# Seven products instead of eight for the output projections of six batches, with all transfers issued by SyncE

## The chip, the core and the metric

The program runs on one core of a Trainium2 chip. The metric is the device time in microseconds of one execution. Three runs of the kernel before gave 1334.11, 1334.73 and 1335.27 us, a median of 1334.73 us. One more execution was taken with the hardware profiler, and all durations below come from it.

Five engines matter here. PE (TensorE) multiplies matrices and writes only to PSUM; PEld is the part of it that loads the stationary operand. DVE (VectorE) and ACT (ScalarE) read and write PSUM and SBUF. POOL (GpSimd) does element-wise work on SBUF only. SP (SyncE) issues transfers. Each engine works through its own instructions in order.

## The reference

Two layers run one after the other on x of shape (8, 512, 512), all in float32. The first is a graph attention over the first 20 tokens of each batch. The second is a self-attention with 16 heads, and the change is in its output projection:

```python
h = _sln(hidden, w, ln_g, ln_b, Wg, bg, Wb, bb)          # conditioned layer norm
qkv = (h @ Wqkv.T + bqkv).reshape(B, N, num_heads, hd, 3)
...
energy = jnp.einsum('bhqd,bhkd->bhqk', q, k)
att = jax.nn.softmax(energy, axis=-1) / D ** 0.5
out = jnp.einsum('bhqk,bhkd->bhqd', att, v)
out = jnp.moveaxis(out, 1, 2).reshape(B, N, D)
out = out @ Wp.T + bp                                    # the output projection
h1 = out + hidden
h2 = _sln(h1, w, ln_g, ln_b, Wg, bg, Wb, bb)
return h2 + h1
```

Here B = 8, N = D = 512, and a head has hd = 32 columns.

## The kernel before

**Stages.** The first layer takes the first 412 us and writes its result to the DRAM tensor `mid`. In it `out_weights` (L435) makes a small tensor per direction and half of the batches, and writes it to the DRAM tensor `vo_d` in four pieces (L448, issued by POOL, 16 pieces in all); `load_vo` (L450, issued by SP) reads it back, 20 pieces per batch. The second layer then takes one batch after the other.

**Steps.** The work of the second layer is a list `steps` (L789). For the batches b = 0 to 6 there are 16 steps, one for each group g of four heads and each block c of 128 queries; `at` (0 to 15) is the number of the step in its batch. A step does, in the order in which the code issues it: the scores of the next step (`scores`, L799, PE) and their row maxima (`tops`, L806, DVE); in steps 1 to 4 the transposition of a quarter of the next batch's tokens (`turn`, tile `pz`); in even steps the products of probabilities and values of two steps (`weigh`, tile `pao`); the exponentials of the next step (`exps`, L811, ACT); the transpositions of this step's probabilities in four parts (`turn_probs`, L824, tile `pt`, three copied out by ACT and one by DVE); a first and a second "job"; and the normalization of the next step's probabilities in two pairs (`normalize`: a reciprocal on DVE at L816, then the scaling of two 128x512 tiles on POOL at L819). In DVE's order each reciprocal stands behind the addition that empties the job before it. The transpositions, the jobs and `turn` share three PSUM banks (`bank`, L651).

**Jobs.** `JOBS` (L869) gives each batch 32 slots, two per step, written out by hand; `None` leaves a slot empty. A job is one of these: half of a group of the plain projection of batch 0 (`own`); one of seven products (`product`, L695) that make Q, K or V of the next batch by the Winograd form of Strassen's method; a product of this kind that is done late (`late`); or one of eight blocks of an output projection (`project`, L731). A product is four matmuls with 256 moving columns. So is one block of `project`: 128 tokens by 256 outputs, summed over four blocks of the 512 inputs, and then added to the residual `XQ[b]` by DVE (L742). The batches 1 to 5 have 29 jobs and three empty slots each: the second slots of the steps 8, 10 and 12. The projection of batch b-1 is done in the steps 1 to 4 of batch b.

**Sums for the products.** Winograd's form needs four sums of quarters of each operand. `weight_sums` (L674) makes those of the weights for V, Q and K once, in the steps 0 to 11 of batch 0, on DVE. `token_sums` (L684) makes those of the tokens in every batch, on POOL, in the steps 2, 4, 4 and 5 (in batch 0 in 3, 4, 4 and 5) at the end of the step.

**The end of a batch.** The last norm of batch b-1 is taken in batch b, in four blocks of 128 tokens, at the steps that `FINISH` (L880) gives: "statistics" (DVE, and a power on POOL) in the steps 2, 3, 4 and 5; "norm" (two operations on DVE, L754 and L755) and "sums" (two additions on POOL, L758 and L759, and the transfer to `out` by SP, L760) in the steps 4, 6, 6 and 8. After that, `fetch` loads the residual of batch b+2 into the buffer that has come free. The bias of the projection is added to the residual by POOL (L115) in the steps 10, 11, 12 and 15.

**Tiles.** `outputs` (L842, ACT) writes the attention's outputs `AO[b, g]` to six tiles of 128x512 (pool `aop`, L642).

Of the kernel before, what the change touches and what calls it, by code (L numbers as in the profile page):

```python
# [9 lines left out]
F32 = mybir.dt.float32  # L10
# [3 lines left out]
ALU = mybir.AluOpType  # L14
# [4 lines left out]
B, N, F = 8, 512, 512  # L19
P = 128  # L20
C = N // P
# [3 lines left out]
NG = 20  # L25
# [4 lines left out]
BH = B // 2  # L30
# [14 lines left out]
def graph_then_self_attention(ctx: ExitStack, tc: tile.TileContext, x, x_t, near, near_t, labels, w_self_t, wq, wk_t,  # L45
                              wout_t, wg_t, wb_t, wqkv_t, wp_t, cols, gate_vecs, rows, out):
    nc = tc.nc
# [27 lines left out]
    turned = ctx.enter_context(tc.tile_pool(name="turned", bufs=2))  # L75
# [12 lines left out]
    XQ, Z, HT, Q, K, V, AO, GATE, STATS, PAIRS = {}, {}, {}, {}, {}, {}, {}, {}, {}, {}  # L88
# [79 lines left out]
    with ExitStack() as l0:  # L168
# [9 lines left out]
        def bank(name):  # L178
            return ps.tile([P, 512], F32, tag="bank", name=name)
# [142 lines left out]
        for k in range(C):  # L322
            for f in range(C):
                o = psk[f // 2][:, f % 2, :2 * MH]
# [16 lines left out]
        first = self_feat_main(0, (0,))  # L341
# [34 lines left out]
        made = kv.tile([P, C, HM], F32, tag="kv", name="made").rearrange("p c m -> p (c m)")  # L376
        nk = B * HG * D2
        kqb = made[:4, 0:nk]
        for d in range(2):
            for g2 in range(2):  # L380
                pk = pair(f"pk_{d}_{g2}")
                for g in (2 * g2, 2 * g2 + 1):
                    o = pk[:, g % 2, :2 * MH]
                    for k in range(C):
                        nc.tensor.matmul(o, WK[d][:, k, g * P:(g + 1) * P], sfk[:, k, :], start=(k == 0), stop=(k == C - 1))
                for g in (2 * g2, 2 * g2 + 1):
                    o = pk[:, g % 2, :2 * MH]
# [47 lines left out]
        def out_weights(d, half, ks):  # L435
            if 0 in ks:
                PW[d, half] = bank(f"pw_{d}_{half}")
            pw = PW[d, half]
            for k in ks:
                nc.tensor.matmul(pw[:MH, :], sfk[:, k, half * MH:(half + 1) * MH], WO[d][:, k, :], start=(k == 0), stop=(k == C - 1))  # L440
            if C - 1 not in ks:
                return

            vot = BOUT[d] if half else (three if d else two).tile([P, KB, P], F32, tag="t" if d else "wt", name=f"vot_{d}").rearrange(
                "p i n -> p (i n)")[:MH, :F]
            nc.vector.tensor_tensor(vot, pw[:MH, :], BOUT[d], ALU.add)
            for b in range(BH):
                nc.gpsimd.dma_start(vo_d[BH * half + b, d], vot[NG * b:NG * (b + 1), :])  # L448

        def load_vo(b):  # L450
            src = vo_d[b].rearrange("d m f -> (d m) f")
# [88 lines left out]
        for n in range(2 * C):  # L540
            d, f = n % 2, n // 2
# [97 lines left out]

    w1 = ctx.enter_context(tc.tile_pool(name="w1", bufs=1, reuse_waits="tile"))  # L640
    qkp = ctx.enter_context(tc.tile_pool(name="qkp", bufs=3, reuse_waits="tile"))
    aop = ctx.enter_context(tc.tile_pool(name="aop", bufs=6, reuse_waits="tile"))  # L642
    gp = ctx.enter_context(tc.tile_pool(name="gp", bufs=1, reuse_waits="tile"))
    op = ctx.enter_context(tc.tile_pool(name="op", bufs=2, reuse_waits="tile"))
    ep = ctx.enter_context(tc.tile_pool(name="ep", bufs=8, reuse_waits="tile"))
# [12 lines left out]
    bv = w1.tile([P, C], F32, name="bv")  # L658
    hx = ctx.enter_context(tc.tile_pool(name="hx", bufs=1, reuse_waits="tile"))

    M = F // 2
    SUMS = {}
# [5 lines left out]
    def a_(i, p, q):  # L671
        return quarter(W1[i], q, p)

    def weight_sums(i, n):  # L674

        if n == 2:
            SUMS[i, 2] = a_(i, 1, 0)
        else:
            SUMS[i, n] = w1.tile([P, 2, M], F32, name=f"s{n + 1}_{i}")
        x0, x1, how = ((a_(i, 1, 0), a_(i, 1, 1), ALU.add), (SUMS.get((i, 0)), a_(i, 0, 0), ALU.subtract),  # L680
                       (a_(i, 0, 0), a_(i, 1, 0), ALU.subtract), (a_(i, 0, 1), SUMS.get((i, 1)), ALU.subtract))[n]
        nc.vector.tensor_tensor(SUMS[i, n], x0, x1, how)

    def token_sums(b, n):  # L684

        SUMS["t", n] = (qk0.tile([P, N], F32, tag="qk"[n], name=f"t{n + 1}_{b}").rearrange("p (k n) -> p k n", k=2) if n < 2
                        else hx.tile([P, 2, M], F32, tag=f"t{n}", name=f"t{n + 1}_{b}"))
        x0, x1 = ((quarter(HT[b], 0, 1), quarter(HT[b], 0, 0)), (quarter(HT[b], 1, 1), SUMS.get(("t", 0))),
                  (quarter(HT[b], 1, 1), quarter(HT[b], 0, 1)), (quarter(HT[b], 1, 0), SUMS.get(("t", 1))))[n]
        nc.gpsimd.tensor_tensor(SUMS["t", n], x0, x1, ALU.subtract)  # L690


    b_less = w1.tile([P, 2, 2], F32, name="b_less")

    def product(b, i, n):  # L695
# [27 lines left out]
        for dst, src in {2: [((0, 0), (1, 0))], 6: [((1, 0), (1, 0))], 5: [((1, 1), (1, 0))], 3: [((0, 1), (1, 1))],  # L723
# [4 lines left out]
            else:  # L728
                nc.vector.tensor_tensor(c_(*dst), out, c_(*src), ALU.add)

    def project(b, c, n):  # L731

        if c == 0 and n == 0:
            pool, tag, shape = (turned, "turned", [P, C, F]) if b == B - 1 else (gp, "gate", [P, 2, F])
            GATE[b] = pool.tile(shape, F32, tag=tag, name=f"gate_{b}")[:, 0:2, :]
            nc.sync.dma_start(GATE[b], gates[b].partition_broadcast(P))
# [105 lines left out]
    def outputs(n):  # L842

        b, g, c = steps[n]
        last = b == B - 1
        at = slice(c * P, (c + 1) * P)
        if c == (0 if last else C - 1):
            if not last:
                AO[b, g] = aop.tile([P, N], F32, tag="ao", name=f"ao_{b}_{g}")
# [12 lines left out]

    def out_of(*cs):
        return [("project", c, n) for c in cs for n in range(2)]
# [8 lines left out]
    JOBS[B - 2][14:] = (made(v, 3) + made(q, 1, 2) + [None] + made(q, 6, 5) + made(k, 1) + [None] + made(k, 2, 6) + made(q, 3) + [None]  # L873
                        + made(k, 5, 3) + made(q, 4, 7) + made(k, 4, 7))
# [16 lines left out]

    def finish_parts(part):
        for block in FINISH.get((b, at), ()):
            if block[2] == part:
                finish(*block)

    def job(b, slot):
        what = JOBS[b][slot] if slot < len(JOBS[b]) else None
        if what is None:
            return  # L900
        kind, *of = what
        if kind == "own":
            i, f, n = of
            if n == 0:
                OWN[0] = q_or_k(i, f)
            OWN[0].half(n)
        elif kind == "product":
            product(b + 1, *of)
        elif kind == "late":
            product(b, *of)  # L910
        else:
            project(*(of if b == B - 1 else [b - 1] + of))

    with tc.manual_schedule():
# [22 lines left out]
        for n, (b, g, c) in enumerate(steps):  # L937
# [129 lines left out]
```

## Time and profile before

| | us |
|---|---|
| median of three runs | 1334.73 (1334.11 to 1335.27) |
| profiled execution | 1335.18 |
| span of its instructions | 1333.40 |
| first layer, 0 to 412.3 | 412.30, PE busy 404.49 |
| batches 0 to 6, 412.3 to 1226.0 | 813.70, PE busy 811.30 |
| batch 7 (another order of steps), 1226.0 to 1333.4 | 107.40, PE busy 98.96 |

The granted clock of PE is 1.00 in all but the last of these, where it is 0.98. The groups of instructions that the change touches, all with 128 partitions in float32:

| line, engine | what | count | mean ns |
|---|---|---|---|
| L740 PE | block of the output projection, 256 columns | 496 records (two per matmul) | 382 |
| L705 PE | one of seven products for Q, K, V, 256 columns | 1568 records | 379 |
| L742 DVE | adds a block to the residual, 128x256 | 62 | 424 |
| L729 DVE | adds a product to a result, 128x512 | 119 | 688 |
| L690 POOL | sum of two quarters of tokens, 128x512 | 28 | 1271 and 1409 |
| L758, L759 POOL | last sums of a block, 128x512 | 31 each | 1288, 1273 |
| L819 POOL | scales probabilities, 128x512 | 511 | 708 |
| L448 POOL | issues a piece of `vo_d` | 16 | 505 to 539 |

How to read it: a matmul's records overlap the next one's, so their busy times don't add up to the time that they take. The chain of waits (the work that ended last, followed back from the last instruction) gives the time that each group really held the end back; there the four matmuls of a job appear as one piece "x8".

### The profile page before, as it was taken

The page shows a single profiled execution, that of the slowest core. Times are in us where ns is not written, and L with a number is a line of the kernel's source. Part 1 is how long each engine was busy: PE and PEld are TensorE (multiplying, and loading weights), DVE is VectorE, ACT ScalarE, POOL GpSimd, SP SyncE. Part 2 cuts the span into 40 slices and gives each one's busy share as a digit, 9 for nine tenths or more (in the row PEclk, how much of TensorE's full clock was granted, in tenths as well). Part 3 has the DMA queues.
Part 4 walks back from the last instruction along what each step waited for, and adds up shares of the span by engine and source line. Part 5 has one row for each costly group of instructions (what it writes and reads, how often), then busy time and mean ns, then how long its engine had stood idle before and what let it go on. Part 6 is the DMA issues. An engine that isn't in the chain of part 4 may idle for free.

```text
span 1333.4 us, 29328 instructions
## 1 busy us (share of the span) xinstructions
PE 1314.7 (99%) x11251; PEld 967.4 (73%) x11251; DVE 943.7 (71%) x1723; ACT 683.2 (51%) x1664; POOL 755.6 (57%) x865
## 2 busy tenths in 40 slices
PE   8999999999999999999999999999999999999997
PEld 5566666666675677777777777777777777777775
DVE  4567777677646578687677768767776875776887
ACT  1322222222225665656656665665666666566664
POOL 0256654555653555486367548636754864674776
PEclk9999999999999999999999999999999999999999
DMA  9614452253221000001002000100200010010010
GB/s 339 204 64 140 166 191 87 97 159 126 89 74 62 2 2 1 2 25 57 1 10 73 2 1 25 57 2 9 73 2 1 25 57 1 9 41 2 10 41 32
DMA packets 46521, 78.63 MB, mean 59 GB/s; under 512 B 9872, under 2 KB 14416, under 8 KB 46384
## 3 DMA queue, kind: packets, MB, share of 16 engines
q1 hardware_dynamic: 45440, 75.57, 16.7%
q8 instruction: 90, 1.47, 0.5%
q0 software_dynamic: 512, 0.66, 0.2%
q10 hardware_dynamic: 432, 0.55, 0.1%
q14 instruction: 47, 0.39, 0.1%
HBM read 59.27 MB, written 17.49 MB: 58 GB/s over the span
## 4 chain that ended last, share of the span: by engine, by line
PE 86%; DVE 8%; POOL 2%; issue 2%; DMA 1%; ACT 1%; POOLq 0%; SPq 0%; DVEq 0%; ACTq 0%
PE pst L705 18%; PE pt L824 16%; PE s L799 9%; PE pss L471 9%; PE pao L839 8%; PE ppj L740 8%; PE psf L300 6%; PE po L515 2%; PE pqk L138 2%; DVE top L806 2%; PE pz L124 1%; PE ptw L503 1%; PE pw L440 1%; PE pq L421 1%; PE pv L138 1%
## 5 line engine op out<-in xcount | busy, mean ns | idle before, releaser
L819 POOL TENSOR_SCALAR e<-e,den 128x512 f32<-128x512 f32 x511 | 361.6, 708 | 340.5 <-DVE den L816 226.0
L811 ACT ACTIVATE e<-s,top 128x512 f32<-128x512 f32 x512 | 348.6, 698 | 132.2 <-DVE top L806 114.7
L806 DVE TENSOR_REDUCE top<-s 128x2 f32<-128x1024 f32 x256 | 301.1, 1218 | 25.5 <-PE s L799 25.0
L824 PEld LDWEIGHTS pt<-ident,e 128*128 128x128 f32 x2048 | 234.3, 141 | 85.2 <-POOL e L819 32.9
L824 PE MATMUL pt<-ident,e 128*128 128x128 f32 x2048 | 290.8, 277 | 3.7 <-ACT et L826 1.6
L826 ACT COPY et<-pt 128x512 f32<-128x512 f32 x369 | 208.8, 595 | 105.1 <-PE pt L824 103.9
L799 PE MATMUL s<-k_pair,q_pair 32*128 32x512 f32 x992 | 143.7, 640 | 0.9
L471 PE MATMUL pss<-kq,sf 128*128 128x320 f32 x512 | 143.2, 433 | 1.0 <-DVE kq L428 1.0
L839 PEld LDWEIGHTS pao<-et,v 128*32 128x32 f32 x4096 | 107.5, 110 | 44.4 <-issue 44.4
L839 PE MATMUL pao<-et,v 128*32 128x128 f32 x4096 | 126.5, 274 | 0.0
L471 PEld LDWEIGHTS pss<-kq,sf 128*128 128x128 f32 x512 | 94.9, 190 | 37.5 <-ACT sf L307 1.5
L740 PE MATMUL ppj<-w,ao 128*128 128x256 f32 x496 | 118.5, 382 | 0.0
L300 PE MATMUL psf<-vt,ws 128*128 128x512 f32 x256 | 115.0, 593 | 0.0
L811 ACT ACTIVATION_READ_ACCUMULATOR e<-s,top 128x1 f32 x512 | 109.6, 214 | 0.0
L826 DVE COPY et<-pt 128x512 f32<-128x512 f32 x143 | 96.7, 677 | 3.1 <-PE pt L824 2.8
L740 PEld LDWEIGHTS ppj<-w,ao 128*128 128x128 f32 x496 | 89.3, 190 | 12.4 <-ACT ht L126 2.8
L497 POOL TENSOR_TENSOR t<-t,den 128x640 f32<-128x640 f32 x32 | 40.7, 1272 | 81.2 <-DVE den L496 80.6
L300 PEld LDWEIGHTS psf<-vt,ws 128*128 128x128 f32 x256 | 48.3, 190 | 50.7 <-issue 46.6
L505 ACT COPY wt<-ptw 128x640 f32<-128x640 f32 x32 | 22.2, 693 | 104.8 <-PE ptw L503 104.4
L742 DVE TENSOR_TENSOR xq<-ppj,xq 128x256 f32<-128x256 f32 x62 | 26.3, 424 | 69.6 <-PE ppj L740 69.6
L126 ACT ACTIVATE ht<-pz,gates_t 128x512 f32<-128x512 f32 x32 | 24.7, 778 | 74.2 <-PE pz L124 74.2
L492 ACT ACTIVATE t<-t 128x640 f32<-128x640 f32 x32 | 23.6, 737 | 76.1 <-POOL t L489 76.1
(237 smaller groups left out, 1949.0 us busy)
## 6 DMA issues: line engine op xcount, KB each, us to landing
x<-in_x SPq DMA_DIRECT2D x8, 1024.0 KB
mid<-x SPq DMA_DIRECT2D x32, 256.0 KB
xq<-mid SPq DMA_DIRECT2D x8, 1024.0 KB
out<-o SPq DMA_DIRECT2D x31, 256.0 KB
vt<-in_x_t SPq DMA_DIRECT2D x7, 1024.0 KB
labels<-in_labels SPq DMA_DIRECT2D x16, 440.0 KB
wq<-in_wq SPq DMA_DIRECT2D x4, 1024.0 KB
gate<-gates SPq DMA_DIRECT2D x8, 512.0 KB
```

The lines of the kernel that those rows point to most:

```text
L300: nc.tensor.matmul(psf[f], ws[:, k, f * P:(f + 1) * P], VT[b][:, k, :], start=(k == 0), stop=(k == C - 1))
L471: nc.tensor.matmul(o, SF[b][:, k, cut], KQ[b][:, k, on], start=(k == 0), stop=(k == C - 1))
L497: nc.gpsimd.tensor_tensor(tv, tv, den.to_broadcast([P, 2 * H, NG]), ALU.mult)
L705: nc.tensor.matmul(out[:, m, :], fixed[:, k, m * P:(m + 1) * P], moving[:, k, :], start=(k == 0), stop=(k == 1))
L740: nc.tensor.matmul(out, AO[b, k][:, c * P:(c + 1) * P], wp[:, k, on], start=(k == 0), stop=(k == C - 1))
L799: nc.tensor.matmul(S[n][j // 2][:, j % 2, :], Q[b, g][on, c * P:(c + 1) * P], K[b, g][on, :], start=True, stop=True)
L806: nc.vector.tensor_reduce(TOP[n][:, 2 * pair:2 * pair + 2], S[n][pair], AX.X, ALU.max, negate=True)
L811: nc.scalar.activation(e, S[n][pair][:, j % 2, :], AF.Exp, bias=TOP[n][:, j:j + 1], accum_out=DEN[n][:, j:j + 1])
L819: engine.tensor_scalar(E[n][j], E[n][j], DEN[n][:, j:j + 1], att_scale, ALU.mult, ALU.mult)
L824: nc.tensor.transpose(pt[:, k * P:(k + 1) * P], E[n][j][:, k * P:(k + 1) * P], ident)
L826: copy(et, pt.rearrange("p (k n) -> p k n", k=C))
L839: nc.tensor.matmul(PAO[b, g][DH * j:DH * (j + 1), at], V[b][:, k, DH * h:DH * (h + 1)], ET[n, j][:, k, :], start=(k == 0), stop=(k == C - 1))
```

## The change

In the projections of the batches 0 to 5 the eight blocks are replaced by seven products of the Winograd form, of half the rows and half the columns each (`output_product`). Numbers 1 and 5 need only the first two head groups, and are done in the batch itself in step 14; the numbers 2, 3, 6, 7 and 4 are done in the steps 1 to 3 of the next batch. The sums of quarters of the attention's outputs (`output_sums`, POOL) are made in step 10 of the batch and in the steps 1, 2 and 3 of the next; two of them overwrite quarters that are no longer needed. The partial sums that several results share are kept in two tiles `y`; POOL adds them to the residual at the end of the steps 14, 2 and 3 (`add_gathered`). `weight_sums` also makes the sums for the projection's weights, in the steps 12 to 15 of batch 0. `JOBS` is written anew: 31 jobs in batch 0, 28 in the batches 1 to 5 and 26 in batch 6, which had 29 each. The empty slots of the batches 1 to 5 are now the second slots of the steps 0, 4, 10 and 12. The token sums move to the steps 3, 4, 5 and 6, ahead of the first job. The statistics of the last norm move to the steps 5, 5, 6 and 7, its norms and sums to 6, 6, 8 and 8. The 16 writes of `vo_d` move from POOL to SP, and the scratch for transfers that POOL issues is cut to 1024 bytes. Batch 7, and the projections of batches 6 and 7, stay as they were.

```diff
-                nc.gpsimd.dma_start(vo_d[BH * half + b, d], vot[NG * b:NG * (b + 1), :])
+                nc.sync.dma_start(vo_d[BH * half + b, d], vot[NG * b:NG * (b + 1), :])
...
-    aop = ctx.enter_context(tc.tile_pool(name="aop", bufs=6, reuse_waits="tile"))
+    aop = ctx.enter_context(tc.tile_pool(name="aop", bufs=3, reuse_waits="tile"))
...
+    hp = ctx.enter_context(tc.tile_pool(name="hp", bufs=1, reuse_waits="tile"))
...
+    def output_sums(b, n):
+        B12 = quarter_of_outputs(b, 0, 1)
+        x0 = quarter_of_outputs(b, *((0, 1), (1, 1), (1, 1), (1, 0))[n])
+        x1 = (quarter_of_outputs(b, 0, 0), SUMS.get(("o", 0)), B12, SUMS.get(("o", 1)))[n]
+        SUMS["o", n] = B12 if n == 2 else quarter_of_outputs(b, 1, 0) if n == 3 else hp.tile([P, 2, M], F32, tag=f"t{n}", name=f"to{n + 1}_{b}")
+        nc.gpsimd.tensor_tensor(SUMS["o", n], x0, x1, ALU.subtract)
...
+    def add_gathered():
+        for residual, y in TO_ADD:
+            nc.gpsimd.tensor_tensor(residual, y, residual, ALU.add)
+        TO_ADD.clear()
+
+    def output_product(b, n):
...
+        out = bank(f"psp_{b}_{n}").rearrange("p (m n) -> p m n", m=2)
+        for m in range(2):
+            for k in range(2):
+                nc.tensor.matmul(out[:, m, :], t[:, k, m * P:(m + 1) * P], a[:, k, :], start=(k == 0), stop=(k == 1))
...
+        if n in (1, 6, 7):
+            before = Y.get(b)
+            Y[b] = hp.tile([P, 2, M], F32, tag="y", bufs=2, name=f"y{n}_{b}")
+            if n == 1:
+                nc.scalar.copy(Y[b], out)
+            else:
+                nc.vector.tensor_tensor(Y[b], out, before, ALU.add)
+            for at_c in {1: ((0, 0),), 6: ((0, 1),), 7: ((1, 0), (1, 1))}[n]:
+                TO_ADD.append((c_(*at_c), Y[b]))
+        for at_c in {2: ((0, 0),), 3: ((0, 1),), 4: ((1, 0),), 5: ((1, 1), (0, 1))}.get(n, ()):
+            nc.vector.tensor_tensor(c_(*at_c), out, c_(*at_c), ALU.add)
...
-    JOBS = {b: (late + out_of(0, 1, 2, 3) if b else own) + made(v, 1, 2, 6, 5, 3, 7, 4) + [None]
-            + made(q, 1, 2) + made(k, 1) + [None] + made(q, 6, 5) + made(k, 2) + [None] + made(k, 6) + made(q, 3) + made(k, 5, 3)
-            + made(q, 4, 7) + [None] for b in range(B - 1)}
+    first, fifth = [("output", 0, 1)], [("output", 0, 5)]
+    end = made(k, 5, 3) + first + fifth + made(q, 4, 7)
+    JOBS = {0: own + made(v, 1, 2, 6, 5, 3, 7, 4) + made(q, 1, 2, 6, 5) + made(k, 1, 2, 6) + [None] + made(q, 3) + end}
+    for b in range(1, B - 1):
+        JOBS[b] = (late[:1] + [None] + late[1:] + [("output", 1, n) for n in (2, 3, 6, 7, 4)] + made(v, 1) + [None]
+                   + made(v, 2, 6, 5, 3, 7, 4) + made(q, 1, 2, 6, 5) + made(k, 1) + [None] + made(k, 2, 6) + made(q, 3) + [None] + end)
...
-        for block, first, second in (((b - 1, 0), 2, 4), ((b - 1, 1), 3, 6), ((b - 1, 2), 4, 6), ((b - 1, 3), 5, 8)) if b < B - 1 else (
+        for block, first, second in (((b - 1, 0), 5, 6), ((b - 1, 1), 5, 6), ((b - 1, 2), 6, 8), ((b - 1, 3), 7, 8)) if b < B - 1 else (
...
-    SUMS_AT = {True: {3: (0,), 4: (1, 2), 5: (3,)}, False: {2: (0,), 4: (1, 2), 5: (3,)}}
+    SUMS_AT = {3: 0, 4: 1, 5: 2, 6: 3}
+    OUTPUT_SUMS_AT = {1: (1, 1), 2: (1, 2), 3: (1, 3), 10: (0, 0)}
...
+            if at in OUTPUT_SUMS_AT:
+                back, i = OUTPUT_SUMS_AT[at]
+                if 0 <= b - back < B - 2:
+                    output_sums(b - back, i)
+            if at in SUMS_AT and not last:
+                token_sums(b + 1, SUMS_AT[at])
             job(b, 2 * at)
...
-            if b == 0 and at < 12:
-                weight_sums((v, q, k)[at // 4], at % 4)
+            if b == 0:
+                weight_sums((v, q, k, 3)[at // 4], at % 4)
...
             finish_parts("sums")
-            for i in SUMS_AT[b == 0].get(at, ()) if b + 1 < B else ():
-                token_sums(b + 1, i)
+            add_gathered()
+
+            if at == 0 and 0 < b < B - 1:
+                load_gate(b - 1)
...
-    nc = bacc.Bacc("TRN2", target_bir_lowering=False, num_devices=1)
+    nc = bacc.Bacc("TRN2", target_bir_lowering=False, num_devices=1, dynamic_dma_scratch_size=1024)
```

More of the change, by code (lines that the diff above doesn't have):

```diff
@@ L674, in weight_sums @@
     def weight_sums(i, n):
-        if n == 2:
+        if n == 2 and i < 3:
             SUMS[i, 2] = a_(i, 1, 0)
@@ L690, in token_sums, with quarter_of_outputs @@
         nc.gpsimd.tensor_tensor(SUMS["t", n], x0, x1, ALU.subtract)
+    def output_sums(b, n):
[4 more added lines that the diff above has]
+        nc.gpsimd.tensor_tensor(SUMS["o", n], x0, x1, ALU.subtract)
+    def quarter_of_outputs(b, p, q):
+        return AO["pair", b, p][:, :, M * q:M * (q + 1)]
     b_less = w1.tile([P, 2, 2], F32, name="b_less")
@@ L729, in product, with c_, load_gate @@
                 nc.vector.tensor_tensor(c_(*dst), out, c_(*src), ALU.add)
+    Y, TO_ADD = {}, []
+    def add_gathered():
[3 more added lines that the diff above has]
+    def output_product(b, n):
+        a = {1: lambda: a_(3, 0, 0), 2: lambda: a_(3, 0, 1), 3: lambda: SUMS[3, 3], 4: lambda: a_(3, 1, 1),
+             5: lambda: SUMS[3, 0], 6: lambda: SUMS[3, 1], 7: lambda: SUMS[3, 2]}[n]()
+        t = {1: lambda: quarter_of_outputs(b, 0, 0), 2: lambda: quarter_of_outputs(b, 1, 0), 3: lambda: quarter_of_outputs(b, 1, 1),
+             4: lambda: SUMS["o", 3], 5: lambda: SUMS["o", 0], 6: lambda: SUMS["o", 1], 7: lambda: SUMS["o", 2]}[n]()
+        out = bank(f"psp_{b}_{n}").rearrange("p (m n) -> p m n", m=2)
+        for m in range(2):
+            for k in range(2):
+                nc.tensor.matmul(out[:, m, :], t[:, k, m * P:(m + 1) * P], a[:, k, :], start=(k == 0), stop=(k == 1))
+        def c_(p, q):
+            return XQ[b][:, 2 * q:2 * q + 2, M * p:M * (p + 1)]
+        if n in (1, 6, 7):
[9 more added lines that the diff above has]
+            nc.vector.tensor_tensor(c_(*at_c), out, c_(*at_c), ALU.add)
+    def load_gate(b):
+        pool, tag, shape = (turned, "turned", [P, C, F]) if b == B - 1 else (gp, "gate", [P, 2, F])
+        GATE[b] = pool.tile(shape, F32, tag=tag, name=f"gate_{b}")[:, 0:2, :]
+        nc.sync.dma_start(GATE[b], gates[b].partition_broadcast(P))
     def project(b, c, n):
         if c == 0 and n == 0:
[L734 to L736 removed]
+            load_gate(b)
         out = bank(f"ppj_{b}_{c}_{n}")[:, 0:M]
@@ L848, in outputs @@
             if not last:
-                AO[b, g] = aop.tile([P, N], F32, tag="ao", name=f"ao_{b}_{g}")
+                if g % 2 == 0:
+                    AO["pair", b, g // 2] = aop.tile([P, 2, N], F32, tag="ao", name=f"ao_{b}_pair_{g // 2}")
+                AO[b, g] = AO["pair", b, g // 2][:, g % 2, :]
             else:
@@ L861, in made @@
         return [("product", i, n) for n in ns]
-    def out_of(*cs):
-        return [("project", c, n) for c in cs for n in range(2)]
     q, k, v = 0, 1, 2
@@ L868, in graph_then_self_attention @@
     late = [("late", k, n) for n in (4, 7)]
-    JOBS = {b: (late + out_of(0, 1, 2, 3) if b else own) + made(v, 1, 2, 6, 5, 3, 7, 4) + [None]
-            + made(q, 1, 2) + made(k, 1) + [None] + made(q, 6, 5) + made(k, 2) + [None] + made(k, 6) + made(q, 3) + made(k, 5, 3)
-            + made(q, 4, 7) + [None] for b in range(B - 1)}
-    JOBS[B - 2][14:] = (made(v, 3) + made(q, 1, 2) + [None] + made(q, 6, 5) + made(k, 1) + [None] + made(k, 2, 6) + made(q, 3) + [None]
-                        + made(k, 5, 3) + made(q, 4, 7) + made(k, 4, 7))
+    first, fifth = [("output", 0, 1)], [("output", 0, 5)]
[4 more added lines that the diff above has]
+                   + made(v, 2, 6, 5, 3, 7, 4) + made(q, 1, 2, 6, 5) + made(k, 1) + [None] + made(k, 2, 6) + made(q, 3) + [None] + end)
+    JOBS[B - 2][14:] = (made(q, 1, 2) + [None] + made(q, 6, 5) + made(k, 1) + [None] + made(k, 2, 6) + made(q, 3) + [None]
+                        + made(k, 5, 3) + made(q, 4) + [None] + made(q, 7) + made(k, 4) + made(k, 7))
     JOBS[B - 1] = [("late", v, 4), None, ("late", v, 7)]
@@ L910, in job @@
             product(b, *of)
+        elif kind == "output":
+            output_product(b - of[0], of[1])
         else:
```

## Prediction

> **What bounds the kernel.** I read the page's busy shares first, then a table of stretches, one per batch, then the chain of waits of one batch, then the rows of the groups that change.
>
> ```profile
> PE 1314.7 (99%) x11251; PEld 967.4 (73%) x11251; DVE 943.7 (71%) x1723; ACT 683.2 (51%) x1664; POOL 755.6 (57%) x865
> 760.94:877.20 116.26, 116.00 (x1149) 90.60 (x1148) 85.29 (x153) 73.67 (x184) 69.46 (x88) 1.00 0.07 24
> ```
>
> The second line is batch 3 from step 0 to step 15: length, then busy time of PE, PEld, DVE, ACT, POOL, then granted clock, DMA share and GB/s. PE is busy 116.00 of 116.26 us; DVE at 73% and POOL at 60% have room on average. The batches 1 to 6 all take 116.1 to 116.4.
>
> A busy PE need not be the bound. The Trainium skill, "Perfetto Trace Analysis", section "Identifying the Most-Contended Engine", calls matmul occupancy a bad measure and takes the share of weight loads instead: here 90.60 / 116.26 = 78%. By that rule a fifth of PE's time could be hidden waiting, and a job taken out could bring as little as nothing. The old kernel holds the test, because it has steps with two jobs and steps with one. Steps 0 and 10 of batch 3, from the chain of waits (start, length, what):
>
> ```profile
> 760.94 1.07 PE s L799 x8
> 762.01 1.89 PE pao L839 x64
> 763.90 1.02 PE pt L824 x8
> 764.92 1.73 PE pst L705 x8
> 766.65 0.44 PE pt L824 x4
> 767.09 1.73 PE pst L705 x8
> 768.82 0.44 PE pt L824 x4
> ...
> 835.80 1.07 PE s L799 x8
> 836.87 1.89 PE pao L839 x64
> 838.75 1.02 PE pt L824 x8
> 839.78 1.73 PE pst L705 x8
> 841.50 0.87 PE pt L824 x8
> 842.38 1.07 PE s L799 x8
> ```
>
> Step 0 runs from 760.94 to 769.25, 8.31 us; step 10, whose second slot is empty, from 835.80 to 842.38, 6.58. The difference is 1.73, a whole job. So a removed job is worth its full 1.73 us in an even step, and I take the row, not the rule. The odd steps have no `pao` and last 6.43; with `pz` a step is 0.59 longer. From these pieces a batch of before is 8 x (8.31 + 6.43) + 4 x 0.59 - 3 x 1.73 = 115.1; it takes 116.26, so about 1.1 us of waits are left in it.
>
> **The matmuls (the gain).** Slots hold 29 jobs in each of batches 0 to 6, 203 in all; afterwards 31 + 5 x 28 + 26 = 197. A block of the projection and one product are both four matmuls of 256 columns: the chain has 1.73 for `pst` and 1.73 to 1.99 for `ppj` (the 1.99 behind `pz`). A product with an attention output as stationary operand is near the row of `pst` with tokens as stationary operand, so 1.73. Six jobs less: -10.4 us. By batch: +3.46 in batch 0, -1.73 in each of 1 to 5, -5.19 in 6. All empty slots of the new order lie in even steps, where the trace shows the full 1.73; in an odd step with one job (4.7 us) ACT, at 5.1 us a step (four exponentials at 0.67, three copies at 0.6, a share of the rest), would have been the bound.
>
> **DVE.** Out per batch: eight additions of 0.42, 3.4 us. In: products 2, 3, 4, 6 and 7 once and 5 twice over PSUM and SBUF, 7 x 0.69 = 4.8 (the row of L729). 85.3 becomes 86.7 of about 114.5 us, with PE in front. ACT gains one copy of 0.60. Four weight sums of 0.67 come to the steps 12 to 15 of batch 0: in step 12 DVE then has 2.36 (tops) + 3 x 1.0 (norm statistics) + 0.67 + 0.88 + 0.62 + 0.3 = 7.8 against PE's 6.58, made up in the lighter step 13. I charge 0.6 once, between 0 and 1.5.
>
> **The moved norms.** Steps 5, 6 and 8 become fuller on DVE. Step 5 gets a second set of statistics (+1.0); DVE waits 0.4 + 0.4 + 0.15 us for others in that step now, so step 6 starts about 0.1 to 0.4 late. Step 6 already has two norms and loses 0.2 to them:
>
> ```profile
> 815.60 0.03 issue
> 815.62 0.63 PE pt L824 x4
> ```
>
> There the third transposition waits for a bank that DVE empties only after both norms. Step 8 gets the same pair: its first product can be emptied at about 829.9 on the old clock, and its bank is wanted at 822.68 + 5.70 + 0.44 + 1.73 = 830.55. So 0 to 0.4 a batch, and I take 0.1: 0.6 in all.
>
> **POOL.** Eight additions or subtractions of 128x512 come to each of the six batches. The rows:
>
> ```profile
> L690 POOL TENSOR_TENSOR t<-ht,t 128x512 f32<-128x512 f32 x14 | 19.7, 1409 | 0.6
> L759 POOL TENSOR_TENSOR o<-o,xq 128x512 f32<-128x512 f32 x31 | 39.5, 1273 | 2.4
> ```
>
> Two sums at 1.27, two at 1.41 and four additions at 1.27 are 10.4 us a batch: 69.5 becomes 79.9, 70%. None stands on the path if the scaling of probabilities behind it in POOL's order is still in time. The tightest place is step 3 to 4. In step 3 POOL ends its second pair of scalings at about 787.0; then come an addition, an output sum and the token sum, 3.95 us, to 791.0, where the next scaling started at 790.5. It is wanted at 792.40 + 1.07 + 0.59 + 1.88 = 795.9, so the delay is free. In step 4: scalings end at 794.2, two additions and a token sum end at 798.2, the next scaling starts at 799.4. In steps 7 and 9 the four last sums run as they do in step 7 now, without a wait of PE. Output sums 2 and 3 are ready well before their products: number 3 at about 789.7, product 4 starts at 790.2. That is the thinnest margin, 0.5 us; if it is missed, at most the length of one POOL operation, 1.3 us a batch.
>
> A rule speaks against this part. The skill's "SBUF — State Buffer", section "Who interferes with whom", says that POOL shares its port pair with DVE as an exclusive lock, taken by a DVE operation in a two-port mode or with two SBUF inputs, and that the second to come waits in full. The trace agrees that they collide: L754 takes 0.54 us in the median and 1.50 at most, L755 0.69 and 1.06. By the rule alone each of the eight operations could block DVE for 1.27, 10.2 us a batch, and DVE would stand at 97 of 114.5. By the rows a norm loses 0.4 us on average now (means 0.79 and 0.85), and the new operations lie in steps 14, 15, 1 to 4 and 10, the norms in 6 and 8. I add nothing.
>
> **Waits that go or come.** K's third product moves from the second slot of step 14 to step 13, so the scores of the next batch no longer wait for DVE:
>
> ```profile
> 752.14 1.74 PE pst L705 x8
> 753.88 0.03 issue
> 753.91 0.50 DVE k_pair L727
> 754.40 0.04 issue
> ```
>
> The 0.57 includes a transposition of 0.44 that PE does there anyway, so 0.13 a batch is won, 0.8 in all. An empty second slot lets the next step wait about 0.1 for the scaled tile (0.37 after step 12); step 8's goes, step 0's comes under the cover of `pz`: nothing.
>
> **SP.** The 16 writes cost SP 0.34 to 0.62 us each (its other stores of results and of `q_d`). Eight stand ahead of `load_vo(0)`, which began at 53.6 and issues for 8.3; the other eight come behind it, ahead of the load of x for batch 2 at 62.0. That load then starts at 66 to 70. Its reader, a row sum on DVE, starts at 92.9, and `vo` is first read at 86.9; both have 17 us or more. POOL loses 8.3 us of issuing where PE waits for nobody. The residual of batch b+2 is fetched about 1.3 us later, still some 15 us ahead of its statistics. Cost 0; uncovered it would be those few us once.
>
> **Sum.** -10.4 + 0.6 + 0.6 - 0.8 = -10.0. On the profiled execution (1335.2, 1.8 of it outside the span) 1325.2; it lies 0.45 above the median, so **1324.7**.
>
> **Rivals.**
> (a) The fuller stretch gives half of it back. For it: step 6 already waits, and one norm that collides costs 0.96 (1.50 - 0.54). One such loss per batch on PE: 6 x 0.96 = 5.8, so 1330.5. Against it: the colliding norm of step 6 met a token sum, which now comes earlier.
> (b) Slower: POOL becomes the bound from step 1 to step 7. Its scalings are in order behind output sums and additions that wait for products, so a late product holds up the scaling, the transposition and the next product. The added POOL time is 10.4 us a batch; from 1.73 / 10.4 = 17% of it reaching PE on, the change loses. At a third: 6 x (3.5 - 1.73) = +10.6, 1345. Against it: idle stretches of 2 to 5 us ahead of the first scaling in most steps.
> (c) More than the jobs: the remaining waits shrink to 0.5 a batch, -3.6 more: 1321.
> (d) The change does not do what it says: the six products overlap badly because the sums overwrite quarters that are read late, so batches of 28 jobs stay at 116: 1335 + 3.5 - 5 = 1333.
>
> **Chances.** Forecast, within 1322 to 1328: 0.70; (a) 0.12; (b) 0.07; (c) 0.07; (d) 0.04. The range 1320.5 to 1331 takes in (a) and (c). A change under 0.2% (2.7 us) can't be told from none. Faster 0.89 (the first, (a) and (c)), same 0.04, slower 0.07.
>
> **What would show it.** Right: batches 1 to 5 at 114.3 to 114.8, batch 0 near 120, batch 6 near 111; jobs at 1.73; PE still busy above 99% of them. Wrong: waits of `pt` for POOL L819 in steps 1 to 7, `psp` waiting for POOL, or gaps ahead of `pt` in steps 6 and 8. The forecast fails first if one POOL operation a batch comes late.

## The result, and the profile after

Four runs of the changed kernel gave 1322.51 to 1323.78 us, a median of 1322.66; four of the kernel before 1334.99. The ratio is 0.9908, with a 95% interval of 0.9896 to 0.9921: 12.3 us or 0.9% faster. The range of 1320.5 to 1331 held it, and 1322.66 lies inside the 1322 to 1328 that the forecast gave for itself, near the lower edge; the forecast of 1324.7 was 2.0 us too high. The profiled execution took 1322.61 us, with a span of 1320.8.

The page's busy shares, and the same table of stretches as before for batch 0, batch 3 and batch 6 (length, then busy time of PE, PEld, DVE, ACT, POOL, clock, DMA share, GB/s):

```profile
PE 1303.7 (99%) x11203; PEld 959.1 (73%) x11203; DVE 945.8 (72%) x1721; ACT 685.9 (52%) x1670; POOL 811.3 (61%) x897
```

```profile
412.20:530.26 118.06, 117.66 (x1057) 84.25 (x1056) 84.21 (x144) 74.91 (x186) 64.90 (x80) 1.00 0.01 2
758.71:872.94 114.23, 114.14 (x1137) 89.18 (x1136) 85.20 (x152) 74.17 (x185) 79.77 (x96) 1.00 0.07 25
1101.41:1213.19 111.78, 111.31 (x1122) 86.34 (x1121) 78.80 (x134) 73.39 (x184) 75.02 (x90) 1.00 0.04 16
```

Batch 3 went from 116.24 to 114.23 (the table below), and PE is busy in all but 0.09 of it. POOL rose from 69.46 to 79.77 us. The weight loads' share, 89.18 / 114.23 = 78%, is what it was: that number didn't see that PE was the bound, before or after. DVE, which was to rise to 86.7 us, stayed at 85.20: the four norms of batch 3 (L754, L805 in the kernel after) took 2.57 us in all where they took 3.54.

Step 0 of batch 3 lost its second job, and with it the whole 1.73 us (chain of waits: start, length, what). It runs from 758.78 to 765.37, 6.59 us where it took 8.31:

```profile
758.78 1.07 PE s L850 x8
759.85 1.89 PE pao L890 x64
761.74 1.02 PE pt L875 x8
762.76 1.73 PE pst L719 x8
764.49 0.87 PE pt L875 x8
765.37 1.13 PE s L850 x8
```

The lengths of all steps, from the start of one step's scores to the next in PE's timeline, show where the time went. Batch 3 stands for the batches 1 to 5, which agree within 0.02 us a step.

| step | 0 | 1 | 2 | 3 | 4 | 5 | 6 | 7 | 8 | 9 | 10 | 11 | 12 | 13 | 14 | 15 | sum |
|---|---|---|---|---|---|---|---|---|---|---|---|---|---|---|---|---|---|
| batch 0 before | 7.21 | 7.10 | 8.88 | 7.10 | 8.88 | 6.43 | 8.30 | 6.43 | 6.58 | 6.90 | 6.58 | 6.90 | 6.58 | 6.73 | 8.52 | 6.43 | 115.55 |
| batch 0 after | 7.22 | 7.10 | 8.87 | 7.11 | 8.87 | 6.43 | 8.31 | 6.42 | 8.31 | 6.43 | 8.31 | 6.43 | 6.83 | 6.69 | 8.31 | 6.42 | 118.06 |
| batch 3 before | 8.31 | 7.13 | 8.89 | 7.13 | 8.89 | 6.43 | 8.53 | 6.43 | 6.58 | 6.54 | 6.58 | 6.54 | 6.58 | 6.73 | 8.52 | 6.43 | 116.24 |
| batch 3 after | 6.58 | 7.19 | 8.90 | 7.12 | 7.17 | 6.62 | 8.31 | 6.43 | 8.31 | 6.42 | 6.58 | 6.55 | 6.58 | 6.74 | 8.31 | 6.42 | 114.23 |
| batch 6 before | 8.31 | 7.13 | 8.89 | 7.13 | 8.89 | 6.43 | 8.53 | 6.43 | 6.58 | 6.72 | 6.58 | 6.54 | 6.58 | 6.73 | 8.32 | 6.42 | 116.21 |
| batch 6 after | 6.58 | 7.19 | 8.89 | 7.12 | 7.17 | 6.62 | 8.31 | 6.43 | 7.26 | 6.43 | 6.83 | 6.43 | 6.83 | 6.43 | 6.83 | 6.43 | 111.78 |

Batch 0 costs 2.51 us more, the batches 1 to 5 save 2.00 each, batch 6 saves 4.43, and batch 7 is the same. With 0.66 us at the start (the first scores of step 0 begin at 412.20 after 412.86) this is 12.59 us, the difference of the two starts of batch 7 (1225.78 and 1213.19).

### The profile page after: what moved, and what is told of

It reads as the page before. It is cut to its first block, busy times and chain, and to the rows that moved or that the text cites. A ratio compares the mean times of both kernels' runs of the same rounds, so it can differ in the third digit from the quotient of the medians.

```text
span 1320.8 us, 29329 instructions
## 1 busy us (share of the span) xinstructions
PE 1303.7 (99%) x11203; PEld 959.1 (73%) x11203; DVE 945.8 (72%) x1721; ACT 685.9 (52%) x1670; POOL 811.3 (61%) x897
## 4 chain that ended last, share of the span: by engine, by line
PE 87%; DVE 7%; POOL 2%; issue 1%; DMA 1%; ACT 1%; POOLq 0%; SPq 0%; DVEq 0%; ACTq 0%
PE pst L719 19%; PE pt L875 17%; PE s L850 10%; PE pss L471 9%; PE pao L890 8%; PE psf L300 6%; PE psp L762 6%; PE po L515 2%; PE pqk L138 2%; DVE top L857 2%; PE pz L124 1%; PE ptw L503 1%; PE pw L440 1%; PE pq L421 1%; PE pv L138 1%
## 5 line engine op out<-in xcount | busy, mean ns | idle before, releaser
L870 POOL TENSOR_SCALAR e<-e,den 128x512 f32<-128x512 f32 x511 | 366.8, 718 | 262.4 <-DVE den L867 168.3
L477 POOL TENSOR_TENSOR t<-t,mask 128x640 f32<-128x640 f32 x32 | 49.4, 1544 | 33.8 <-issue 30.2
L489 POOL TENSOR_TENSOR t<-t,top 128x640 f32<-128x640 f32 x32 | 40.7, 1273 | 38.4 <-DVE top L488 38.4
L488 DVE TENSOR_REDUCE top<-t 128x32 f32<-128x640 f32 x32 | 26.2, 818 | 44.3 <-POOL t L481 44.2
```

Of the source, the lines that this page charges most:

```text
L477: nc.gpsimd.tensor_tensor(t, t, MASK[b][:, c, None].to_broadcast([P, H, D2]), ALU.mult)
L870: engine.tensor_scalar(E[n][j], E[n][j], DEN[n][:, j:j + 1], att_scale, ALU.mult, ALU.mult)
```

## Experiments

Each ratio compares runs on one chip, and the kernel before took 1335.08 us on the first (`before_sp`, `before_t3`, `before_k3`, `after_odd`), 1335.53 on the second (`after_again`, `after_late_sum`, `after_pool`, `after_slots`) and 1335.13 on the third (`before_t3_late`, `after_again2`, `after_swap`). The step lengths come from each run's own trace.

**Only the transfers.**

```diff
-                nc.gpsimd.dma_start(vo_d[BH * half + b, d], vot[NG * b:NG * (b + 1), :])
+                nc.sync.dma_start(vo_d[BH * half + b, d], vot[NG * b:NG * (b + 1), :])
...
+    nc = bacc.Bacc("TRN2", target_bir_lowering=False, num_devices=1, dynamic_dma_scratch_size=1024)
```

> The kernel before, with only the transfer part of the change: the 16 writes of vo_d issued by SP, the scratch for POOL's transfers cut to 1024 bytes. My theory (the 0.66 us by which the first layer was shorter in the trace of after is chance in the landing of the first load of x_kv): within 0.5 us of before, batches of 116.2 us. Rival (the move to SP takes 0.7 us out of the start by itself): about 1334.2, and x_kv lands at 17.0 us again in place of 17.7.

Measured: 1335.09 us, ratio 1.0000 (0.9992 to 1.0008). The scores of step 0 begin at 413.19, later than in any other trace here (412.20 to 413.12). SP issued the writes and the late load of x in the same order as in the changed kernel (start, length, queue, line, what):

```profile
48.99 4.88 SPq L448 DMA_DIRECT2D vo_d<-vot  x8
54.57 7.63 SPq L458 DMA_DIRECT2D vo<-vo_d  x20
62.30 3.90 SPq L448 DMA_DIRECT2D vo_d<-bout  x8
66.72 0.41 SPq L205 DMA_DIRECT2D x<-in_x  x1
```

The two groups take 0.61 and 0.49 us a write on average, and x starts at 66.7, inside the 66 to 70 of the prediction. Nothing waits for it. The interval alone would still leave room for 0.7 us; the traces do not. With the same transfers the changed kernel itself began step 0 at 412.20, 413.06 and 413.12 in three traces, so the 0.66 us at the start are chance. Which load they come from stays open: x_kv is read from 17.6 us on here, and from 16.7 in the trace that begins step 0 at 413.12, so it is not this load alone. (SP now issues all transfers but the three that ACT issued before and still does.)

**The fourth token sum, moved within POOL's order by nothing.**

```diff
-    SUMS_AT = {True: {3: (0,), 4: (1, 2), 5: (3,)}, False: {2: (0,), 4: (1, 2), 5: (3,)}}
+    SUMS_AT = {True: {3: (0,), 4: (1, 2)}, False: {2: (0,), 4: (1, 2)}}
...
+            if at == 6 and not last:
+                token_sums(b + 1, 3)
             job(b, 2 * at)
```

> The kernel before, with only the fourth token sum moved from the end of step 5 to step 6 ahead of the first job. Theory (step 6 waited 0.22 us because this sum on POOL and the norm on DVE collided, and that is where batches gained more than the job): step 6 falls from 8.53 to 8.31 us in batches 1 to 6, 1.3 us in all, 1333.5; a norm (L754) no longer takes 1.5 us there. Rival (step 6 was relieved by the lighter DVE work of the new job order): step 6 stays at 8.53, 1334.8.

Measured: 1335.12, ratio 0.9999 (0.9991 to 1.0007), and step 6 stayed at 8.53. That looked like the rival's answer, but the trace shows that the edit didn't test it. The timelines of DVE and POOL in step 6 of batch 3:

```profile
811.06 1.06 DVE L755 TENSOR_TENSOR o<-o,gate 128x512 f32<-128x512 f32 x1
812.05 1.49 DVE L754 TENSOR_SCALAR o<-xq,mv_h 128x512 f32<-128x512 f32 x1
...
811.66 1.59 POOL L690 TENSOR_TENSOR t<-ht,t 128x512 f32<-128x512 f32 x1
```

The end of step 5 and the start of step 6 are the same place in POOL's order: behind the second pair of scalings. The sum met the norm as before. A second edit puts it where it can't.

**The fourth token sum in step 7.**

```diff
-    SUMS_AT = {True: {3: (0,), 4: (1, 2), 5: (3,)}, False: {2: (0,), 4: (1, 2), 5: (3,)}}
+    SUMS_AT = {True: {3: (0,), 4: (1, 2)}, False: {2: (0,), 4: (1, 2)}}
...
+            if at == 7 and not last:
+                token_sums(b + 1, 3)
             job(b, 2 * at)
```

> The kernel before, with only the fourth token sum moved to step 7, ahead of the first job. The earlier run before_t3 didn't test its theory: the end of step 5 and the start of step 6 are the same place in POOL's order, and the sum met the norm of step 6 again (1.59 us beside a norm of 1.49). Here POOL does it behind the last sums of step 6. Theory (the collision of sum and norm holds up DVE, and with it a bank): the norms of step 6 take 0.54 and 0.69, step 6 falls from 8.53 to 8.31 us in batches 0 to 6 where it waited, 1.3 us in all, 1333.7. Rival (two norms ahead of the product's addition are enough for the wait, whatever POOL does): step 6 stays at 8.53, 1335.1.

Measured: step 6 fell to 8.31 in the batches 1 to 6, as the theory says. DVE's timeline in that step:

```profile
811.76 1.06 DVE L755 TENSOR_TENSOR o<-o,gate 128x512 f32<-128x512 f32 x1
812.74 0.54 DVE L754 TENSOR_SCALAR o<-xq,mv_h 128x512 f32<-128x512 f32 x1
```

The norm takes 0.54 us again. (The multiplication before it still takes 1.06, beside a scaling on POOL.) So a DVE operation that met POOL's sum held up PE by 0.22 us through a bank. But the kernel took 1336.11, ratio 1.0007 (0.9999 to 1.0016), and by the trace a batch became 0.18 us longer: step 8 grew from 6.58 to 6.99, since POOL, with the sum behind four others, was late for the scaling there:

```profile
823.39 1.27 POOL L690 TENSOR_TENSOR t<-ht,t 128x512 f32<-128x512 f32 x1
824.75 3.63 POOL L819 TENSOR_SCALAR e<-e,den 128x512 f32<-128x512 f32 x4
```

PE's chain in step 8 runs through this scaling. Taking a collision away is a gain only where POOL's work finds another free place.

**K's fifth and third products one slot earlier.** Q's third product takes the slot behind them.

```diff
-            + made(q, 1, 2) + made(k, 1) + [None] + made(q, 6, 5) + made(k, 2) + [None] + made(k, 6) + made(q, 3) + made(k, 5, 3)
+            + made(q, 1, 2) + made(k, 1) + [None] + made(q, 6, 5) + made(k, 2) + [None] + made(k, 6) + made(k, 5, 3) + made(q, 3)
```

> The kernel before, with only K's fifth and third product done one slot earlier (Q's third product takes the slot behind them). Theory (step 14 waited 0.22 us for DVE's addition of K's third product): step 14 falls from 8.53 to 8.31 us in batches 0 to 5, 1.3 us in all, 1333.5. Rival (any product of two DVE additions in that slot holds up the scores, or the wait comes from the norms of step 14): step 14 stays at 8.53, or the wait moves to step 15; 1334.8.

Measured: 1333.82, ratio 0.9990 (0.9984 to 0.9997), 1.26 us. Step 14 fell from 8.52 to 8.31 in the batches 0 to 5 and nothing else moved: 6 x 0.21 = 1.3. Where the chain of waits passed through an addition on DVE before (the lines in the prediction), PE now goes on (end of step 14):

```profile
757.65 1.73 PE pst L705 x8
759.38 0.44 PE pt L824 x4
759.82 1.07 PE s L799 x8
```

**The empty slots in odd steps.**

```diff
-        JOBS[b] = (late[:1] + [None] + late[1:] + [("output", 1, n) for n in (2, 3, 6, 7, 4)] + made(v, 1) + [None]
-                   + made(v, 2, 6, 5, 3, 7, 4) + made(q, 1, 2, 6, 5) + made(k, 1) + [None] + made(k, 2, 6) + made(q, 3) + [None] + end)
+        JOBS[b] = (late + [("output", 1, 2)] + [None] + [("output", 1, n) for n in (3, 6, 7, 4)] + made(v, 1, 2, 6) + [None]
+                   + made(v, 5, 3, 7, 4) + made(q, 1, 2, 6, 5) + made(k, 1, 2, 6) + [None] + made(q, 3) + end[:2] + [None] + end[2:])
```

> The kernel after, with the four empty slots of batches 1 to 5 in the odd steps 1, 5, 11 and 13 in place of the even steps 0, 4, 10 and 12; the same 28 jobs in the same order. Theory (a job taken out is worth its 1.73 us only where PE still ends last; in an odd step the exponentials and copies of ACT, about 5.1 us, take over from PE's 4.7): the even steps grow by 1.73 each, the odd steps shrink by 1.2 to 1.4 only, 1.3 to 2 us lost a batch, 1329 to 1333. Rival (PE alone counts, wherever the slot is empty): 1322.7.

Measured: 1341.06, ratio 1.0044 (1.0029 to 1.0059): slower than the kernel before, with the same 28 jobs. The direction was right, but the loss is 3.1 us a batch where 1.3 to 2 were expected. An odd step with one job did shrink by the full 1.73, from 6.43 to 4.70 (with `pz`, in step 1, it takes 5.39 where 7.12 is usual); then the next even step took 9.23 in place of 8.31. The first 14 slots of batch 6 are moved along, so it loses 2.3 us too. The chain at the end of step 13, the last exponential there, and the waits of PE's weight loads in the batches 2 to 5 (engine, tile, whom it waits for: us in all, times, longest):

```profile
866.30 0.87 PE pt L875 x8
867.17 1.99 PE s L850 x8
869.16 1.88 PE pao L890 x64
```

```profile
867.18 0.71 ACT L862 ACTIVATE e<-s,top 128x512 f32<-128x512 f32 x1
```

```profile
PEld s L850 <- ACT e L862: 9.8, 16, 0.6
```

PE is ready for the next scores at 867.17 but needs the PSUM tiles that ACT's exponentials still read; the last exponential ran from 867.18 to 867.89. The scores take 1.99 us where they take 1.07: 0.92 lost, in four places a batch (0.83 in step 2). In an odd step ACT copies two transposed tiles ahead of the four exponentials, so it ends last. The rival, PE alone, is out.

**The output sum behind the token sum in step 3.**

```diff
-    SUMS_AT = {3: 0, 4: 1, 5: 2, 6: 3}
+    SUMS_AT = {4: 1, 5: 2, 6: 3}
...
+            if at == 3 and not last:
+                token_sums(b + 1, 0)
             if at in OUTPUT_SUMS_AT:
```

> The kernel after, with the token sum of step 3 ahead of the output sum of step 3 in POOL's order, so that output sum 4 ends 1.27 us later. In the trace of after it ends at 786.04 and product 4 starts at 786.41. Theory (the margin is 0.37 us, and past it PE waits in full): step 3 grows from 7.12 to about 8.0 in batches 1 to 6, 6 x 0.9 = 5.4 us, 1328. Rival (POOL has enough room that the order of its work doesn't matter): 1322.7.

Measured: 1330.22, ratio to before 0.9960 (0.9946 to 0.9974), 7.3 us above the kernel after on the same chip (1322.96). Step 3 grew from 7.12 to 8.29 in the batches 1 to 6. In the kernel after the sum ends at 786.04, and product 4 begins at 786.41 (the first two lines); here the chain runs through POOL (the other four):

```profile
784.77 1.27 POOL L701 TENSOR_TENSOR ao_pair<-ao_pair,to 128x512 f32<-128x512 f32 x1
...
786.41 1.73 PE psp L762 x8
```

```profile
787.46 1.22 POOL t L693
788.68 1.24 POOL ao_pair L701
789.92 0.04 issue
789.96 1.99 PE psp L762 x8
```

A delay of 1.27 us on POOL cost PE 1.17, so the true margin is about 0.1 us. The visible gap of 0.37 isn't all room: in the late run the product begins 0.04 after the sum but takes 1.99 in place of 1.73, so 0.30 of the gap goes whatever POOL does.

**Almost as much POOL work again.** `zero` is a column of zeros; the bias row keeps its values.

```diff
...
             add_gathered()
+            if 1 <= at <= 9 and 0 < b < B - 1:
+                nc.gpsimd.tensor_tensor(bp_bc, bp_bc, zero.to_broadcast([P, F]), ALU.add)
```

> The kernel after, with one more POOL operation of 128x512 (it adds zero to the bias row, about 1.27 us) at the end of each of the steps 1 to 9 of batches 1 to 6: 11.4 us of POOL work more a batch, as much as the change added. Theory (only the place of POOL's work in its order counts; the margin of output sum 4 at step 3, 0.37 us, is the first to go, then the scaling in steps 4 and 7 to 9): 0.9 us at step 3 and up to 1 us in each of the steps 4, 7, 8 and 9: 1328 to 1340. Rival 1 (POOL has 30% idle time and hides it): 1322.7. Rival 2 (POOL was on the edge of being the bound): more than half of the 68 us shows, over 1357.

Measured: 1346.74, ratio to before 1.0084 (1.0069 to 1.0099). The added operation was shorter than the 1.27 us expected:

```profile
L1068 POOL TENSOR_TENSOR bp_bc<-bp_bc,zero 128x512 f32<-128x512 f32 x54 | 56.2, 1041 | 2.4
```

So 56 us were added and not 68, 9.4 a batch. The kernel took 23.8 us more than after, 42% of that: above the theory's 1340, and still less than the half that rival 2 asks for. In the batches 1 to 5 the steps 3, 6, 8, 10 and 11 grew by 0.95, 0.5, 1.3, 0.5 and 0.7; the others didn't. POOL was still only 76% busy in batch 3 (its fifth busy time, as above):

```profile
766.78:884.90 118.12, 115.33 (x1137) 89.09 (x1136) 86.52 (x152) 74.58 (x185) 89.46 (x106) 1.00 0.07 24
```

In step 3 the chain is the one just seen, with the added operation in front:

```profile
791.61 1.27 POOL xq L750
792.88 1.00 POOL bp_bc L1068
793.88 1.24 POOL ao_pair L701
795.11 0.04 issue
795.16 1.99 PE psp L763 x8
```

Step 6 grew for another reason. There the added operation pushed the token sum onto DVE's multiplication, which takes 0.69 alone:

```profile
815.99 1.65 DVE L807 TENSOR_TENSOR o<-o,gate 128x512 f32<-128x512 f32 x1
...
815.63 1.46 POOL L693 TENSOR_TENSOR t<-ht,t 128x512 f32<-128x512 f32 x1
```

So the first 10.3 us a batch were free and the next 9.4 cost 3.9, in part through POOL's order and in part through such meetings with DVE. The change used up most of POOL's room.

**Three moves in the job lists.** Q's third product and K's sixth change places in the batches 1 to 5; in the batches 0 and 6 the empty slots move to second slots (the line for batch 0 is left out here).

```diff
-                   + made(v, 2, 6, 5, 3, 7, 4) + made(q, 1, 2, 6, 5) + made(k, 1) + [None] + made(k, 2, 6) + made(q, 3) + [None] + end)
+                   + made(v, 2, 6, 5, 3, 7, 4) + made(q, 1, 2, 6, 5) + made(k, 1) + [None] + made(k, 2) + made(q, 3) + made(k, 6) + [None] + end)
...
-    JOBS[B - 2][14:] = (made(q, 1, 2) + [None] + made(q, 6, 5) + made(k, 1) + [None] + made(k, 2, 6) + made(q, 3) + [None]
-                        + made(k, 5, 3) + made(q, 4) + [None] + made(q, 7) + made(k, 4) + made(k, 7))
+    JOBS[B - 2][14:] = (made(q, 1, 2, 6) + [None] + made(q, 5) + made(k, 1, 2) + [None] + made(q, 3) + made(k, 6, 5) + [None]
+                        + made(k, 3) + made(q, 4, 7) + [None] + made(k, 4, 7))
```

> The kernel after, with three small moves in the job lists: Q's third product out of the step with an empty slot (K's sixth takes its place), the empty slots of batch 6 in the second slots of the even steps 8, 10, 12 and 14 in place of the first, the one of batch 0 likewise. Theory (a product of two DVE additions in a step with an empty slot makes the next step wait 0.2 us longer; an empty first slot costs 0.1 more than an empty second one; batch 6 loses 0.7 us in step 8): step 13 falls from 6.74 to 6.54 in batches 1 to 5 (-1.0 us), batch 6 loses 1.0 and batch 0 0.3: 1320.4. Rival (the waits come from elsewhere, the norm statistics of step 12): step 13 stays at 6.74, 1321.5 to 1322.7.

Measured: 1323.22, no better than after (1322.96). Step 13 fell from 6.73 to 6.54 in the batches 1 to 5 as expected, 0.9 us. Batch 6, which was to lose 1.0, took it back: 112.37 for 111.59, with steps 9 and 15 at 7.20 and 7.14. At step 15 the edit itself is to blame: it put Q's seventh product, of two DVE additions too, ahead of an empty slot (step 14), and the chain runs through these additions (1.29) and the scaling behind them. In batch 0 step 12 fell from 6.83 to 6.58, but step 13 grew from 6.69 to 7.05; why isn't shown. The kernel after ran again beside the second and the third group:

> The kernel after, unchanged, as the measure for the three below on the same chip: 1322.7, batches 1 to 5 at 114.2 us.

> The kernel after, unchanged, as the measure for the next run on the same chip: 1322.9, step 13 at 6.73 us in batches 1 to 5.

They gave 1322.96 and 1323.22, with the batches 1 to 5 at 114.20 and 114.21.

**The one move that held.** The first of the three alone (the first hunk of the diff above).

> The kernel after with only that part of after_slots that held there: in batches 1 to 5 Q's third product and K's sixth change places. Batches 0 and 6 as in after. Theory: step 13 at 6.54 in place of 6.73, 5 x 0.19 = 0.9 us off, 1322.0, the fastest of all. Rival (one step's gain is taken back by another, as in batch 6 of after_slots): 1322.9.

Measured: 1322.18 (1321.84 to 1322.33) against 1323.22 (1322.34 to 1323.58) for after, ratio to before 0.9903 (0.9887 to 0.9920). Step 13 is 6.54 in five batches and nothing else moved, 0.95 us by the trace. It is the fastest version here, by an amount that the trace shows more surely than the times do.

## Why the prediction was right, and which terms were mis-sized

**The jobs (-10.4).** Right in place and size. A removed job is 1.73 us: steps 0 and 4 of the batches 1 to 6 lost exactly that, step 8 of the batches 1 to 5 gained it back, and so did steps 8 and 10 of batch 0. The weighing of the row against the rule on weight loads came out for the row. The condition that the prediction attached, even steps only, is what `after_odd` confirms; but the reason was drawn too simply. The odd step itself isn't bound by ACT; the wait falls on the next scores, and costs 0.92 and not 0.4.

**K's third product (-0.8).** Right mechanism; the term of 0.13 us a batch was too small: 0.21, six times, by `before_k3`. The prediction took the transposition of 0.44 off a wait of 0.57, but it left out that the scores behind the wait take longer, 1.14 us for 1.07:

```profile
754.45 1.14 PE s L799 x8
```

With these 0.07 the term is 0.20.

**The fuller stretch (+0.6).** The prediction let it cost 0.1 a batch; steps 5, 6 and 8 together went from 21.54 to 23.24, 1.70 for a job of 1.73, so it cost nothing, and rival (a) is out. Step 5 grew by 0.19 behind the step with an empty slot (the scaled tile came late) and step 6 lost its 0.22. `before_t3_late` shows that this 0.22 can go by keeping POOL's sum off the norm, and `after_pool` that step 6 waits again when the sum is pushed back onto DVE's work. That the change itself gains it in the same way is read from its trace, not isolated: the two norms of step 6 take 0.58 and 0.54 there, and the mean of all norms fell from 791 to 611 ns:

```profile
805.99 0.58 DVE L805 TENSOR_SCALAR o<-xq,mv_h 128x512 f32<-128x512 f32 x1
...
807.21 0.54 DVE L805 TENSOR_SCALAR o<-xq,mv_h 128x512 f32<-128x512 f32 x1
```

```profile
L754 DVE TENSOR_SCALAR o<-xq,mv_h 128x512 f32<-128x512 f32 x31 | 24.5, 791 | 0.0
```

```profile
L805 DVE TENSOR_SCALAR o<-xq,mv_h 128x512 f32<-128x512 f32 x31 | 18.9, 611 | 0.1
```

The prediction had this reason in hand, as its argument against rival (a), and gave it no weight in the sum. So the lock rule that the prediction quotes, which spoke against the change, tells what a collision costs (the last section has the times); what it can't say is where collisions fall, and here more work on POOL met DVE less often.

**Batch 0 (+3.46 and +0.6).** The two jobs are there. Step 12 grew by 0.25, but not for the weight sum that the prediction charged: the steps 10, 12 and 14 of batch 6, which have an empty first slot like it and no weight sum, take 6.83 too, where a step with an empty second slot takes 6.58, and with the second slot empty (`after_slots`) step 12 of batch 0 is back at 6.58. Behind an empty first slot twelve transpositions run in a row, and the product after them takes longer (step 10 of batch 6):

```profile
1176.43 1.46 PE pt L875 x12
1177.90 1.98 PE pst L719 x8
```

What the prediction missed: steps 9 and 11 each lost a wait of 0.47, which had followed the empty slots of steps 8 and 10. The chain went through POOL's scaling there, slowed beside a weight sum on DVE: four scalings in 3.40 us where they take 3.04 elsewhere.

```profile
479.69 0.67 DVE L682 TENSOR_TENSOR s<-w 128x512 f32<-128x512 f32 x1
...
479.86 3.40 POOL L819 TENSOR_SCALAR e<-e,den 128x512 f32<-128x512 f32 x4 [3.72 <-PE pt L824]
```

Step 14 lost the 0.21 of K's third product. So batch 0 cost 2.51, and not the 3.9 to which the prediction's terms add up.

**Batch 6 (-5.19).** It saved 4.43. Three jobs went; the empty first slots cost 0.25 each in the steps 10, 12 and 14 and 0.7 in step 8, where the chain runs through POOL's scalings behind the two DVE additions of Q's second product. Against that, steps 9, 11 and 13 lost waits of 0.7 in all. The prediction charged nothing for the first slots. Step 8 isn't steady: in the two other traces of this kernel it takes 6.95 and step 10 takes 6.98, and the batch 111.6.

**POOL and rival (b).** The prediction's 79.9 us of POOL a batch became 79.77, and its 0.5 us of margin at output sum 4 became 0.37 to look at and 0.1 in truth. The prediction named this as the thinnest place; `after_late_sum` and `after_pool` show that it was the nearest to rival (b). That rival's price, a third of the added work, is near what the next portion costs (42%).

**Rivals (c) and (d).** By the prediction's own pieces a batch of 28 jobs is 113.36 us, so 0.87 of waits are left in 114.23 where about 1.1 were: (c) came true by about half. (d) is out, since the batches of 28 jobs did not stay at 116.

**SP, at nothing.** Confirmed by `before_sp`.

**How good the hit was.** The terms are -0.66 by chance, +2.51, -10.01 and -4.43, against a sum of -10.0 (+3.9, -8.8 and -5.1 when the small terms are given to their batches). Batch 0 came out 1.4 better, the batches 1 to 5 together 1.2 better and batch 6 0.7 worse. Of the signs that were to show it right, jobs at 1.73 and PE above 99% came true; the batches 1 to 5 lie just below the 114.3 to 114.8, and batch 0, at 118.06, well below 120. The 10.4 us of the jobs are no luck. That the median fell inside 1322 to 1328 owes something to it: it lies 0.66 us above the lower end, about as much as batch 6 came out worse.

## What to carry to other kernels

Where one engine ends every step, look for steps of the old kernel that already lack the work in question: their length prices its removal better than any busy share. Where the freed slot stands matters as much as that it is freed: the same 28 jobs took 1322.7 or 1341.1 us. And work given to an engine with idle time is free only as far as its place in that engine's order: ask which operation behind it is due first, and by how much.

## What was not expected of the hardware

A DVE norm of 0.54 us beside a POOL sum of 1.27 became 1.49 and the sum 1.59. In the lines of `before_t3` the sum runs from 811.66 to 813.25 and the norm from 812.05 to 813.54: the norm ended 0.29 us after the sum that was ahead of it. The multiplication of `after_pool` ended 0.55 after the sum that it met (817.64 against 817.09). The norm lost 0.95 of the 1.20 us that were left of the sum when it began, the multiplication 0.96 of 1.10: nearly all of it, as the lock rule has it. That the sum too was longer fits the multiplication ahead of the norm, which ran until 812.12; no run here isolates it.

And a POOL operation that ends 0.37 us ahead of the matmul which needs its result leaves only about 0.1 us to spare.
